# Chunked scan: head states packed into 112 rows by 96 channels, with the states' outputs computed by two row tiles

## The chip, the cores and the metric

The kernel runs on one core of a Trainium2 chip. A core has five engines that work side by side and wait for each other through semaphores: TensorE (PE, matmuls from SBUF into PSUM), VectorE (DVE), ScalarE (ACT), GpSimd (POOL, which in this kernel works on SBUF only) and SyncE (SP, which here issues nearly all transfers). PSUM is used in eight banks of 512 fp32 values per partition. The metric is the device time of one launch in microseconds, for a batch of eight images. The kernel before took 30100.37 us (median of 3 runs, 30061.18 to 30136.38).

## The reference, cut to what matters

Four layers work on x of shape (8, 64, 64, 96), each as `x = x + layer(group_norm(x))`. Layers 0 and 2 are selective scans, layer 3 is a spectral layer. The change concerns layer 1 alone, a chunked scan over the 4096 tokens in four directions k (rows, columns, and both reversed), with 6 heads of 32 channels (192 in all) and a state of 16 values. For one chunk of tokens t, s and one head h:

```python
cum  = cumsum(dt * A)                              # per head, within the chunk
Wt   = (C[t] . B[s]) * tril(exp(cum[t]-cum[s])) * dt[s]
y_intra = einsum('bctsh,bcshd->bcthd', Wt, xr)
S_loc   = einsum('bcsh,bcshn,bcshd->bchdn', decay_end * dt, Brh, xr)
state   = exp(cum[last]) * state + S_loc           # from chunk to chunk
y_inter = einsum('bcth,bcthn,bchdn->bcthd', exp(cum), Crh, prev_states)
y = y_intra + y_inter + xr * Dp
```

So a state belongs to one head: 16 state values by that head's 32 channels. The products of one head's state values with another head's channels are never used.

## The kernel before, in words

The batch is worked image by image, and an image layer by layer. `chunked_scan` (L711) does layer 1: the convolution, then two orders (`chunked_order`, L744), o = 0 for row order and o = 1 for column order, each with its forward and its reversed direction (i = 0 and 1). So the code below runs 16 times in a launch. Chunks have Q = 128 tokens, so an order has 32 chunks per direction.

The first half of an order ("turn") projects B, C and dt, transposes x into `xt` (tokens on partitions) and so on. The second half (from L843) is the chunk loop. Its order of work is written out by hand (`tc.manual_schedule()`): what a step emits is what each engine executes, in that order. Step n works on two items at once, the forward chunk n and the reversed chunk 31 - n, and each stage runs ahead of the next (L1075 to L1085):

- `decays(n+1)`, ACT: for each item, absolute value and exponential of `sg` in PSUM (L952, L953), which gives `wt` in SBUF, 128 x 768; POOL makes `xdt` (L957).
- `outputs(n)`, PE: for each item and each half of the channels (hf), three matmuls `wt`, `xdt` into 32-row column groups of `py` (L1022), and then one matmul of the state with `ce` that is added to the same 96 rows (L1030). `py` is one bank.
- `shares(n+1)`, PE: for each item one matmul, `bw` (6 heads x 16 state values, 96 columns) by all 192 channels of `xt` (L972) into `st`, 96 x 192. This computes every head against every channel.
- `sums(n+2)`, PE: four matmuls into `sg` (L936), by row tiles of 32 rows, one of each item side by side; POOL makes `bw` (L924). `sg` has two buffers of two banks, one for each item, so that these matmuls need the exponentials of `decays(n+1)` done.
- parts of two "quads". A quad prepares what four chunks need, in four parts that are run in four successive steps: `pl` (PE, L872); then its copy `lr` (ACT, L881), `rr` (POOL, L883) and `cb` (PE, L892); then `cbm` (DVE, L895) and `pd` (PE, L899); then `ec` (ACT, L904) and `ce` (POOL, L906). `pl`, `cb` and `pd` take turns in a pool of two banks (L847). In the steady part of the loop a step with `pd` and `pl` alternates with a step with `cb`. The last four steps of an order have no quad part that uses PE.
- `weights(n+1)`, DVE: `wt` times `cbm` for each item (L984).
- `add_y(n)`, DVE: adds `py` into y (L1046 in the first half of order 0, else L1060).
- `advance(n+1)`, DVE: for each item `own` = `st` times a mask that keeps each head's own channels (L1001), and the new state = old state times the chunk's decay plus `own` (L1003), both 96 x 192. The state that `outputs` uses is that of the `advance` of the step before.

The state's rows are (head, state value) and its columns all 192 channels, with zeros where the head of the row isn't that of the channel, so that one matmul of all 96 rows gives the sum over heads.

`py`, `st` and `xdt`: `py` and `st` have a single buffer, so `outputs(n+1)` waits for `add_y(n)`, and `shares` for the `own` of the step before. The eight banks are: quad pool two, `sg` four, `py` one, `st` one.

Of the kernel before, what the change touches and what calls it, by code (L numbers as in the profile page):

```python
# [9 lines left out]
F32 = mybir.dt.float32  # L10
# [7 lines left out]
DM = 96  # L18
NST = 16
# [8 lines left out]
Q = 128  # L28
NQ = L // Q
HID = 384  # L30


C_IN = 0
# [21 lines left out]
K_LW = K_UB + 128  # L55
K_DIA = K_LW + 2 * LWC
K_S6 = K_DIA + 6
K_BLK = K_S6 + 4 * 96
K_UP = K_BLK + 192
K_DN = K_UP + 128  # L60
K_ALL = K_DN + 64

# [2 lines left out]
def tile_vision_stack(  # L65
# [645 lines left out]
    def chunked_scan(w, d, u, y):  # L711

        xproj = w[:, C_XP : C_XP + K * 2 * XR].rearrange("p (k j r) -> p k j r", k=K, j=2)
        yr = y.rearrange("p j (h w) -> p j w h", w=64)
        with tc.tile_pool(name="both", bufs=1) as bo, tc.tile_pool(name="bcd", bufs=1, space=DRAM) as bdp:
            cc = bo.tile([128, K_UP - K_TF], F32, name="cc")
            nc.sync.dma_start(cc, consts[:, K_TF:K_UP])
            lw_fixed = cc[:, K_LW - K_TF : K_DIA - K_TF].rearrange("p (i r) -> p i r", i=2)
            lw = bo.tile([128, 2, NQ, LWC], F32, name="lw")  # L730
            for i in range(2):
                (nc.gpsimd.tensor_copy if i else nc.vector.tensor_copy)(
                    lw[:, i, :, :], lw_fixed[:, i : i + 1, :].to_broadcast([128, NQ, LWC])
                )

            bts = [bo.tile([DM, 4 * Q], F32, name=f"bt{n}") for n in range(2)]
            for bt in bts:
                nc.gpsimd.memset(bt, 0.0)
            bcds = [bdp.tile([32, L], F32, name=f"bcd{k}") for k in range(K)]
            for o in range(2):  # L740
                with tc.tile_pool(name="order", bufs=1) as op:
                    chunked_order(o, w, d, xproj, u, y, yr, cc, lw, bts, bcds, op)

    def chunked_order(o, w, d, xproj, u, y, yr, cc, lw, bts, bcds, op):  # L744
        def part(at, n):
            return cc[:, at - K_TF : at - K_TF + n]

        tris = (part(K_TF, 128), part(K_TB, 128))
        past = (part(K_UF, 128), part(K_UB, 128))
        heads = part(K_DIA, RK)  # L750
        sel6 = part(K_S6, 4 * 96).rearrange("p (j m) -> p j m", j=4)
        same = part(K_BLK, 192)[:DM]
        xt = op.tile([128, NQ, 192], F32, name="xt")
        xd = op.tile([128, NQ, 2, RK + NST], F32, name="xd")
        dt = op.tile([128, NQ, 2, RK], F32, name="dt")
# [87 lines left out]
        with (  # L843
            tc.tile_pool(name="quad", bufs=3) as qp,
            tc.tile_pool(name="chunk1", bufs=4) as cp,
            tc.tile_pool(name="state1", bufs=3) as stp,
            tc.tile_pool(name="p_quad", bufs=2, space=PSUM) as pqp,  # L847
            tc.tile_pool(name="p_seg", bufs=2, space=PSUM) as psg,
            tc.tile_pool(name="p_y", bufs=1, space=PSUM) as pyp,
            tc.tile_pool(name="p_st", bufs=1, space=PSUM) as pst,  # L850
# [2 lines left out]
            quads = {}  # L853
            count = [0]

            def quad(i, base):

                m = quads[i, base] = {}
                here = slice(base * Q, (base + 4) * Q)
                src = bcds[o + 2 * i]  # L860
                bt = bts[count[0] % 2]
                count[0] += 1
                nc.sync.dma_start(bt[:NST], src[:NST, here])

                cr = qp.tile([DM, 4 * Q], F32, name="cr", bufs=2)
                for h in range(RK):
                    nc.sync.dma_start(cr[NST * h : NST * h + NST], src[NST:, here])

                pl = pqp.tile([128, 2, 256], F32, name="pl", tag="quad")
                for part, at in ((0, RK), (1, 0)):  # L870
                    for j in range(4):
                        nc.tensor.matmul(  # L872
                            pl[32 * j : 32 * j + 32, part, :Q],
                            lw[:, i, base + j, at : at + 32],
                            tris[i],
                            start=True,
                            stop=True,
                        )
                yield
                m["lr"] = lr = qp.tile([128, 2, Q], F32, name="lr", bufs=4)  # L880
                nc.scalar.copy(lr, pl[:, :, :Q])  # L881
                m["rr"] = rr = qp.tile([128, RK, Q], F32, name="rr")
                nc.gpsimd.tensor_mul(  # L883
                    rr,
                    lr[:, 1:2, :].to_broadcast([128, RK, Q]),
                    heads.unsqueeze(2).to_broadcast([128, RK, Q]),
                )

                cb = pqp.tile([128, 4, Q], F32, name="cb", tag="quad")
                for j in range(4):  # L890
                    at = slice(j * Q, j * Q + Q)
                    nc.tensor.matmul(cb[:, j, :], bt[:, at], cr[:, at], start=True, stop=True)  # L892
                yield
                m["cbm"] = cbm = qp.tile([128, 4, Q], F32, name="cbm", bufs=4)
                nc.vector.tensor_mul(cbm, cb, tris[i].unsqueeze(1).to_broadcast([128, 4, Q]))  # L895

                pd = pqp.tile([128, 4, Q], F32, name="pd", tag="quad")
                for j in range(4):
                    nc.tensor.matmul(  # L899
                        pd[:DM, j, :], sel6[:, j, :], lr[:, 0, :], start=True, stop=True  # L900
                    )
                yield
                m["ec"] = ec = qp.tile([DM, 4, Q], F32, name="ec")
                nc.scalar.activation(ec, pd[:DM], AF.Exp)  # L904
                m["ce"] = ce = qp.tile([DM, 4, Q], F32, name="ce", bufs=4)
                nc.gpsimd.tensor_mul(ce, ec, cr.rearrange("p (j t) -> p j t", j=4))  # L906

            items = []
# [54 lines left out]
            def shares(n):  # L963

                if "bw" not in live[n]:
                    return
                st = pst.tile([DM, 2, 192], F32, name="st")
                for e in (n, n + 1):
                    i, c = items[e]
                    it = live[e]  # L970
                    it["st"] = st[:, i, :]
                    nc.tensor.matmul(  # L972
                        st[:, i, :],
                        it["bw"].rearrange("p h n -> p (h n)"),
                        xt[:, c, :],
                        start=True,
                        stop=True,
                    )

            def weights(n):  # L980
                for e in (n, n + 1):
# [8 lines left out]
            def advance(n):  # L990
                for e in (n, n + 1):
# [1 line left out]
                    m, j, it = quads[i, c - c % 4], c % 4, live[e]  # L993
                    it["before"] = states[i]
                    if "st" in it:
                        new = stp.tile([DM, 192], F32, name=f"state{i}")
                        if states[i] is None:
                            nc.vector.tensor_mul(new, it["st"], same)
                        else:
                            own = stp.tile([DM, 192], F32, name="own", bufs=1)  # L1000
                            nc.vector.tensor_mul(own, it["st"], same)  # L1001
                            last = Q - 1 if i == 0 else 0
                            nc.vector.scalar_tensor_tensor(  # L1003
                                new,
                                states[i],
                                m["ec"][:, j, last : last + 1],
                                own,
                                ALU.mult,
                                ALU.add,
                            )  # L1010
                        states[i] = new

            def outputs(n):
                py = pyp.tile([DM, 2, 2, Q], F32, name="py")
                for e in (n, n + 1):
                    i, c = items[e]
                    m, j, it = quads[i, c - c % 4], c % 4, live[e]
                    it["py"] = py[:, i, :, :]
                    for hf in range(2):
                        for q in range(3):  # L1020
                            h = 3 * hf + q
                            nc.tensor.matmul(  # L1022
                                py[32 * q : 32 * q + 32, i, hf, :],
                                it["xdt"][:, h, :],
                                it["wt"][:, h, :],
                                start=True,
                                stop=it["before"] is None,
                            )
                        if it["before"] is not None:
                            nc.tensor.matmul(  # L1030
                                py[:, i, hf, :],
                                it["before"][:, 96 * hf : 96 * hf + 96],
                                m["ce"][:, j, :],
                                start=False,
                                stop=True,
                            )
# [202 lines left out]
def _constants():  # L1239
# [15 lines left out]
        c[edge, K_LW + i * LWC + 2 * RK : K_LW + i * LWC + 3 * RK] = 1  # L1255
    h = np.arange(RK)
    c[:, K_DIA : K_DIA + RK] = (m[:, None] % 32 < 2 * RK) & (m[:, None] % 32 % RK == h)
    for j in range(4):
        c[:, K_S6 + 96 * j : K_S6 + 96 * j + 96] = r == 32 * j + s[:, :96] // NST
    c[:DM, K_BLK : K_BLK + 192] = r[:DM] // NST == np.arange(192)[None, :] // 32  # L1260
    c[:DM, K_GRP : K_GRP + 96] = (r[:DM] // 3 == s[:, :DM] // 3) / 3.0

    f = np.minimum(m, 128 - m)
# [120 lines left out]
```

## Time and profile before

| | us |
|---|---|
| median of 3 runs | 30100.37 (30061.18 to 30136.38) |
| the profiled execution | 30160.23 |
| its span, first to last instruction | 30158.4 |
| busy over the span: PE, DVE, POOL, ACT | 23685.8, 24821.0, 21704.5, 16367.5 |
| mean granted TensorE clock | 0.754 |
| L1022 on PE, `wt` and `xdt`, x12288 | 854.5 busy |
| L1030 on PE, state and `ce`, x3968 | 920.2 busy |
| L972 on PE, `bw` and `xt`, x1984 | 410.3 busy |
| L1003 on DVE, new state, x960 | 575.7 busy |
| L1001 on DVE, own share, x960 | 335.8 busy |

A group of the profile is named by line, engine and operation, then output and inputs; "busy" is the time in which at least one of its instructions ran. An fp32 matmul of the code stands as two instructions in the trace (the 3968 rows of L1030 are 1984 calls). Ends of matmuls are modelled and overlap, so what a matmul takes of PE is read from one start to the next. A "window" is a stretch of the span in us. The chunk loops of the first image lie at about 1531 to 1736 us and 1797 to 2004 us; the other seven images repeat them.

### The profile page before, as it was taken

What the parts mean: (1) busy time and instruction counts of PE and PEld (TensorE: products, weight loads), DVE (VectorE), ACT (ScalarE), POOL (GpSimd) and SP (SyncE); (2) the same over time, 40 slices, a digit from 0 to 9 for tenths busy, and PEclk for the clock granted to TensorE, in tenths of its full rate; (3) what the DMA queues carried; (4) which work ended last, traced back from release to release, by engine and by line L of the source; (5) the groups of instructions that cost most, each with busy time, mean ns of one, the idle gap of its engine ahead of it and who ended that gap; (6) DMA issues with size and microseconds to landing.
All of it is one profiled execution on the core that took longest, in us unless ns stands there. A gap on an engine that the chain in (4) does not pass through costs nothing. (4 is left out here: it accounts for less than half of the span.)

```text
span 30158.4 us, 279416 instructions
## 1 busy us (share of the span) xinstructions
PE 23685.8 (79%) x90246; PEld 8903.9 (30%) x90246; DVE 24821.0 (82%) x17921; ACT 16367.5 (54%) x28493; POOL 21704.5 (72%) x8844
## 2 busy tenths in 40 slices
PE   7797877978779787797877978779787797877978
PEld 1141412414124141241412414124141241412414
DVE  9879698796987969879698796987969879698796
ACT  5546465464654646546465464654646546465464
POOL 8749487594875948759497594975949759487594
PEclk7687777867768777787777877768777687776877
DMA  5415253152541525415253152531525315253152
GB/s 124 96 35 132 61 124 92 38 131 59 123 94 37 132 58 123 95 37 132 61 123 92 40 132 57 124 92 40 132 58 124 92 39 131 58 124 93 38 132 60
DMA packets 1503971, 2689.40 MB, mean 89 GB/s; under 512 B 305624, under 2 KB 313144, under 8 KB 1502512
## 3 DMA queue, kind: packets, MB, share of 16 engines
q1 hardware_dynamic: 1485872, 2665.23, 37.6%
q8 instruction: 723, 11.85, 0.2%
q10 hardware_dynamic: 16640, 6.29, 0.1%
q14 instruction: 736, 6.03, 0.1%
HBM read 2287.51 MB, written 383.06 MB: 89 GB/s over the span
## 5 line engine op out<-in xcount | busy, mean ns | idle before, releaser
L569 DVE TENSOR_TENSOR_SCAN h<-da,db 128x1026 f32<-128x1026 f32 x6144 | 13729.5, 2281 | 504.0 <-PE py L607 163.8
L590 POOL TENSOR_TENSOR h<-h,c 128x2048 f32<-128x2048 f32 x3072 | 12746.6, 4175 | 146.6 <-ACT state L585 142.4
L533 PE MATMUL pu<-du,cst 32*128 32x512 f32 x4096 | 3240.4, 881 | 3524.5 <-DVE db L539 3499.4
L554 ACT ACTIVATE da<-dx,a0s 128x512 f32<-128x512 f32 x6144 | 4243.4, 691 | 2592.1 <-DVE h L569 2431.3
L554 ACT ACTIVATE da<-dx,a2s 128x512 f32<-128x512 f32 x6144 | 4243.5, 691 | 2589.6 <-DVE h L569 2433.0
L607 PE MATMUL py<-h,cst 128*32 128x512 f32 x24576 | 5415.8, 811 | 68.0 <-POOL h L590 68.0
L539 POOL TENSOR_TENSOR db<-du,b 128x2048 f32<-128x2048 f32 x1024 | 4650.6, 4542 | 580.1 <-ACT db L525 580.1
L539 DVE TENSOR_TENSOR db<-pu,b 128x2048 f32<-128x2048 f32 x2048 | 4642.2, 2267 | 6.3 <-issue 6.3
L607 PEld LDWEIGHTS py<-h,cst 128*32 128x32 f32 x24576 | 1180.7, 145 | 4967.1 <-issue 4529.5
L229 POOL TENSOR_SCALAR xn<-xs,sb 96x512 f32<-96x512 f32 x192 | 203.1, 1062 | 3191.2 <-DVE sb L209 3050.5
L533 PEld LDWEIGHTS pu<-du,cst 32*128 32x128 f32 x4096 | 802.0, 243 | 5542.9 <-DVE db L539 3999.3
L455 PE MATMUL pv<-u,wk 96*128 96x512 f32 x2048 | 1774.1, 1008 | 760.9 <-ACT raw L451 760.9
L446 PE MATMUL pv<-u,wk 96*96 96x512 f32 x2048 | 1480.9, 852 | 515.3 <-ACT state L585 245.0
L597 PE MATMUL py<-y,cst 96*96 96x512 f32 x1536 | 1551.1, 1108 | 403.8 <-ACT raw L460 363.6
L952 ACT ACTIVATE sg<-sg 128x768 f32<-128x768 f32 x1024 | 820.5, 801 | 1400.3 <-PE sg L936 1400.3
L498 POOL TENSOR_TENSOR du<-raw,u 96x512 f32<-96x512 f32 x1024 | 1442.2, 1430 | 0.0
L984 DVE TENSOR_TENSOR wt<-wt,cbm 128x768 f32<-128x768 f32 x1024 | 1022.9, 1004 | 492.1 <-ACT wt L953 491.8
L585 ACT COPY state<-h 128x4 f32<-128x4 f32 x3072 | 607.6, 198 | 1157.3 <-DVE h L569 1157.3
L1146 DVE SCALAR_TENSOR_TENSOR f<-p,w3bs,f 128x512 f32<-128x512 f32 x768 | 576.7, 751 | 719.6 <-ACT f L1139 693.0
L906 POOL TENSOR_TENSOR ce<-ec,cr 96x512 f32<-96x512 f32 x256 | 405.0, 1582 | 976.2 <-ACT ec L904 966.0
L455 PEld LDWEIGHTS pv<-u,wk 96*128 96x128 f32 x2048 | 535.8, 289 | 1921.9 <-ACT raw L451 1444.1
L883 POOL TENSOR_TENSOR rr<-lr,cc 128x768 f32<-128x768 f32 x256 | 375.7, 1468 | 1001.2 <-ACT lr L881 813.5
(210 smaller groups left out, 32525.8 us busy)
## 6 DMA issues: line engine op xcount, KB each, us to landing
dx<-dd SPq DMA_DIRECT2D x4096, 192.0 KB, 3.8
b<-bcd SPq DMA_DIRECT2D x2048, 256.0 KB, 5.2
c<-bcd SPq DMA_DIRECT2D x2048, 256.0 KB, 6.5
du<-dud SPq DMA_DIRECT2D x2048, 128.0 KB, 2.7
dd<-raw SPq DMA_DIRECT2D x1024, 192.0 KB, 5.3
dud<-du SPq DMA_DIRECT2D x512, 128.0 KB, 1.9
xd<-xs SPq DMA_DIRECT2D x256, 192.0 KB, 2.1
xs<-xd SPq DMA_DIRECT2D x128, 384.0 KB, 5.7
```

Source lines behind the costliest of these rows:

```text
L446: nc.tensor.matmul(pv[:DM], weights[k][:, hi, 128:], uv[hi], start=(hi == 0), stop=(hi == 1))
L455: nc.tensor.matmul(pv, weights[k][:, hi, :128], uv[hi], start=(hi == 0), stop=(hi == 1))
L498: nc.gpsimd.tensor_mul(cut(du[:, hf, :], wh), cut(delta[hf], wh), uv[hf])
L533: nc.tensor.matmul(pu, sel[rows, :], m["du"][rows, n // 3, :], start=True, stop=True)
L539: (nc.gpsimd if pool else nc.vector).tensor_mul(groups(m["db", n]), (m["du2"][:, n // 3, :] if pool else m["pu"]) .unsqueeze(1) .to_broadc ...
L554: nc.scalar.activation(dst[:, g, :LC], made[i]["dx"][n // 3][:, n % 3, :], AF.Exp, scale=av4[:, k, n, gs : gs + 1],)
L569: nc.vector.tensor_tensor_scan(made[i]["h", n][:, at][:, way], das[p][:, rev : 2 * SEG + rev][:, way], made[i]["db", n][:, at][:, way], 0. ...
L590: nc.gpsimd.tensor_mul(h, h, made[i]["c"])
L597: nc.tensor.matmul(py, skip[:, hf, :] if k == 0 else ident[:DM, :DM], view((u if k == 0 else y)[:, hf, :], wh, c * LC, LC), start=True, st ...
L607: nc.tensor.matmul(py[32 * q : 32 * q + 32, :], red, hs[q][:, g, :], start=False, stop=(g == NSG - 1),)
L952: nc.scalar.activation(sg, sg, AF.Abs)
L984: nc.vector.tensor_mul(it["wt"], it["wt"], m["cbm"][:, j : j + 1, :].to_broadcast([128, RK, Q]),)
```

## The change

States become 112 rows by 96 channels. Rows 0 to 47 hold heads 0 to 2 (channels 0 to 95), rows 64 to 111 hold heads 3 to 5 (channels 96 to 191), and rows 48 to 63 stay zero. With that:

- `shares` makes four matmuls in place of two: for each item and half 48 columns of `bw` by that half's 96 channels, into rows 0 to 47 and 64 to 111.
- `advance` works on 112 x 96 in place of 96 x 192.
- `outputs` makes all six `wt`/`xdt` matmuls of an item first, and then two matmuls of state and `ce`, each of 48 rows (0 to 47, and 64 to 111), into the two halves of `py`, which now lie in two different banks.
- `ec`, `ce`, `pd`, `cr` and `bt` get the same 112 rows (`cr` becomes a pair of fixed buffers, cleared once per image, as `bt` was), by constants that are laid out anew.
- The banks are shared out anew: `py` has two; `st` and `pl` lie in one bank together (`pst2`, cleared once per order by DVE); `cb` and `pd` have one bank between them (`bufs=1`).

The diff, cut to its core:

```diff
-            bts = [bo.tile([DM, 4 * Q], F32, name=f"bt{n}") for n in range(2)]
-            for bt in bts:
-                nc.gpsimd.memset(bt, 0.0)
+            bts = [bo.tile([HR, 4 * Q], F32, name=f"bt{n}") for n in range(2)]
+            crs = [bo.tile([HR, 4 * Q], F32, name=f"cr{n}") for n in range(2)]
+            for t in bts + crs:
+                nc.gpsimd.memset(t, 0.0)
...
-            tc.tile_pool(name="p_quad", bufs=2, space=PSUM) as pqp,
+            tc.tile_pool(name="p_quad", bufs=1, space=PSUM) as pqp,
...
+            pst2 = pst.tile([128, 512], F32, name="pst2")
+            nc.vector.memset(pst2, 0.0)
+            sts = pst2[:HR, :192].rearrange("p (i c) -> p i c", i=2)
+            pl = pst2[:, 256:].rearrange("p (a t) -> p a t", a=2)
...
-                pl = pqp.tile([128, 2, 256], F32, name="pl", tag="quad")
...
-                        pd[:DM, j, :], sel6[:, j, :], lr[:, 0, :], start=True, stop=True
+                        pd[:HR, j, :], sel6[:, j, :], lr[:, 0, :], start=True, stop=True
...
-                    it["st"] = st[:, i, :]
-                    nc.tensor.matmul(
-                        st[:, i, :],
-                        it["bw"].rearrange("p h n -> p (h n)"),
-                        xt[:, c, :],
-                        start=True,
-                        stop=True,
-                    )
+                    it["st"] = sts[:, i, :]
+                    for hf in range(2):
+                        nc.tensor.matmul(
+                            sts[64 * hf : 64 * hf + 48, i, :],
+                            it["bw"].rearrange("p h n -> p (h n)")[:, 48 * hf : 48 * hf + 48],
+                            xt[:, c, 96 * hf : 96 * hf + 96],
+                            start=True,
+                            stop=True,
+                        )
...
-                            own = stp.tile([DM, 192], F32, name="own", bufs=1)
+                            own = stp.tile([HR, 96], F32, name="own", bufs=1)
...
-                py = pyp.tile([DM, 2, 2, Q], F32, name="py")
+                py = pyp.tile([DM, 2, 4 * Q], F32, name="py")
+                py = py.rearrange("p j (i t) -> p j i t", i=4)
...
+                    for hf in range(2):
                         if it["before"] is not None:
+                            rows = slice(64 * hf, 64 * hf + 48)
                             nc.tensor.matmul(
-                                py[:, i, hf, :],
-                                it["before"][:, 96 * hf : 96 * hf + 96],
-                                m["ce"][:, j, :],
+                                py[:, hf, i, :],
+                                it["before"][rows, :],
+                                m["ce"][rows, j, :],
                                 start=False,
                                 stop=True,
                             )
```

## The prediction

> **What bounds the kernel now.** I first asked where the code of the change runs and which engine is never idle there. The windows view of two stretches inside the chunk loops of one image, one of each order (columns: us, then busy time and instructions of PE, PE's weight loads, DVE, ACT, POOL, then granted clock, DMA share, GB/s):
>
> ```profile
> 1604.00:1655.00 51.00, 51.00 (x481) 31.66 (x480) 40.83 (x82) 27.91 (x41) 30.47 (x41) 1.00 0.09 20
> 1844.00:1895.00 51.00, 51.00 (x481) 31.63 (x481) 42.98 (x69) 27.91 (x41) 30.32 (x41) 1.00 0.08 20
> ```
>
> The page's whole-span averages (DVE 82%, PE 79%) hide this: here PE is busy 51.00 of 51.00 us at full clock, DVE 80 to 84%, ACT 55%, POOL 60%. A busy PE can be one that crawls, so next I read PE's timeline over one pair of steps (start us, us to the modelled end of the last, what; no line carries a bracket with idle time):
>
> ```profile
> 1603.29 0.42 PE L1022 MATMUL py<-wt,xdt 128*32 128x128 f32 x6
> 1603.64 0.46 PE L1030 MATMUL py<-ce,state 96*96 96x128 f32 x2
> 1604.03 0.42 PE L1022 MATMUL py<-wt,xdt 128*32 128x128 f32 x6
> ...
> 1606.15 0.82 PE L972 MATMUL st<-xt,bw 128*96 128x192 f32 x4
> 1606.89 1.56 PE L936 MATMUL sg<-rr,lr 32*128 32x384 f32 x8
> 1608.38 1.11 PE L899 MATMUL pd<-lr,cc 128*96 128x128 f32 x8
> 1609.43 0.64 PE L872 MATMUL pl<-cc,lw 128*32 128x128 f32 x16
> 1609.89 0.40 PE L1022 MATMUL py<-wt,xdt 128*32 128x128 f32 x6
> ...
> 1614.96 1.16 PE L892 MATMUL cb<-cr,bt 96*128 96x128 f32 x8
> 1616.05 0.31 PE L1022 MATMUL py<-wt,xdt 128*32 128x128 f32 x3
> ```
>
> From start to start: the step with `pd` and `pl` takes 6.60 us, the one with `cb` 6.16, the pair 12.76. Single starts repeat to 0.01 us from group to group, which waiting on another engine would not do. So each us taken off PE here is gained, until the next ring of waits binds. The last four steps of an order, without quads, take 5.10 us each. An order has 13 pairs, one short first step and those four; there are 16 orders.
>
> The next limit is seen on the other two engines in the same pair, ACT and DVE (in brackets the idle time before, and what ended it):
>
> ```profile
> 1608.48 0.80 ACT L952 ACTIVATE sg<-sg 128x768 f32<-128x768 f32 x1 [3.00 <-PE sg L936]
> ...
> 1610.86 0.81 ACT L953 ACTIVATE wt<-sg 128x768 f32<-128x768 f32 x1
> ...
> 1610.16 0.96 DVE L984 TENSOR_TENSOR wt<-wt,cbm 128x768 f32<-128x768 f32 x1 [0.83 <-ACT wt L953]
> 1611.70 0.96 DVE L984 TENSOR_TENSOR wt<-wt,cbm 128x768 f32<-128x768 f32 x1 [0.59 <-ACT wt L953]
> 1612.93 1.12 DVE L1046 SCALAR_TENSOR_TENSOR y<-u,d,py 96x128 f32<-96x128 f32 x4 [0.27 <-PE py L1030]
> 1613.97 0.35 DVE L1001 TENSOR_TENSOR own<-st,cc 96x192 f32<-96x192 f32 x1
> 1614.42 1.02 DVE L1003 SCALAR_TENSOR_TENSOR state<-state,ec,own 96x192 f32<-96x192 f32 x1
> ```
>
> ACT waits 3.00 us for PE's sums. ACT's ring is: sums' start to first absolute value 1.59 us (1606.89 to 1608.48), four activations 3.19 (to 1611.67), about 0.07 hand-over to the next sums: 4.85 us per step.
>
> **What the Trainium skill says.** TensorEngine Tiling, Key Properties: changing the tiling mode drains the array. The trace agrees: the last L1022 start to the first L1030 start is 0.202 us, where a 128-column pass without a mode change takes 0.109. TensorE: Matmul & The Clock Gate, LDWEIGHTS: a load costs its columns over 1.2 GHz, so 80 ns for 96; in the trace the second pass after a mode change comes at 0.187, that is 0.109 + 0.078. The same page, The mechanism: tiles on different rows run side by side. L936 does it here with 32-row tiles: two 384-column passes start 7 ns apart and the next two 0.322 later, the time of one. No row shows 64-row tiles. SBUF — State Buffer, section "SBUF: two separate sides": DVE and POOL share a port pair as an exclusive lock; L1003 fits it, with 0.415 us median, 0.600 mean and 1.672 at most.
>
> **The change part by part.**
>
> Outputs. Now an item costs 2 x (0.35 + 0.39) = 1.48 us: four mode changes. After: six L1022 matmuls are four bursts of three passes, which by the bursts of `pl` start at 0, 0.134, 0.243, 0.352, the last pass at 0.366; mode change 0.202; two passes of both row tiles side by side, 0.187 + 0.007; mode change 0.202. Sum 0.964 per item, 1.93 per step.
>
> Shares. Four 192-column passes now take 0.162 each; with the mode change before the sums, 0.74 from 1606.15. After: 96-column passes, by the slope between 128 (0.109) and 192 columns (0.162), 0.082. Two column tiles side by side make four pairs: 0.122 with the first load of 48 columns, 0.082, 0.082, 0.007, then 0.175 to the sums: 0.47.
>
> Outputs and shares together: 3.60 now (1603.29 to 1606.89), 2.40 after: 1.20 to 1.21 us per step. `pd` with 112 weight columns and `cb` with 112 rows keep their passes.
>
> The pair on PE alone: 12.76 - 2.42 = 10.34. Against ACT's 2 x 4.85 = 9.70 PE still binds. In the four steps without quads PE would need 3.89, so ACT binds: 4.85, a gain of 0.25 each.
>
> DVE. `own` and the new state lose 96 elements per row. The slope from `own` (192 elements, 0.35) to L984 (768, 0.96) is 1.07 ns per element, so 0.10 us each, 0.40 per step. Alone this is off the path.
>
> New waits. In the built program dependences in `pst2` are held for the bank, not the columns. So in the step with `pl`, DVE's first `own` waits for `pl`, the last work of PE's step; behind it on DVE stand the other three of `advance`, then the next step's L984 twice and L1060, and for that `outputs` waits (`py` has one buffer). That closes a ring, per pair: from the end of `pl`, `advance` 1.23 (1.63 now from 1607.70 to 1609.33 on DVE, less 0.40), two L984 2.0, add 1.1 to 1.2, hand-overs 0.15; then PE's outputs 1.93, shares 0.47, sums 1.49, `pd` 1.04, `pl` 0.36 to its last start and 0.28 to its end. Sum 10.1 to 10.2, just under PE's 10.34, with nothing for the port lock. With the mean of L1003, 0.2 to 0.4 more: 10.3 to 10.6. I take 10.55 for the pair.
>
> The single quad bank: `pd` waits for `cbm`, `cb` for `ec`. In the steady loop `cbm` ends at 1604.7 and `pd` starts at 1608.38, so 3.7 us cover it; `cb` waits for `ec` already with two banks, since three tiles rotate. Before the loop `pd` starts at 1525.92 and `cbm` ends at 1526.86: about 1.0 us later, once per order, on the path. ACT's `lr` and the `own` of the other step wait for each other's reads with over a us to spare. `rr` and `ce` follow `ec` and `lr` at 1.5 us each on POOL and are needed 1.6 us or more later. Two more 0.52 us clears on POOL lie before 96.69 us of its idling; that of `pst2` is on DVE while it waits for PE.
>
> Sum per order: 13 x (12.76 - 10.55) = 28.7; four steps 1.0; first step 0.3; start -1.0: 29.0 us. Times 16: 464 us. The profiled execution (30160) becomes 29696; the median of the runs lies 60 below it, so 29636, say 29640.
>
> What no row prices: which bank the next order's first matmuls wait for (`py`'s second bank is freed last), -2 to +2 us per order, so up to 32 us each way; I take 0.
>
> **The rivals.**
>
> *The row tiles don't overlap.* Then the state matmuls cost 2 x 0.109 more per item, 0.44 per step; the gain per step falls to 0.77. For it: no 64-row tile in the trace. Against it: L936. 26 x 0.77 + 1.3 - 1.0 = 20.3 per order: 29775.
>
> *DVE becomes the bound* by the ring above. If one state update in each `advance` is stretched (2.52 us from 1613.97 to 1616.49 now, 2.1 after) and L984 pairs take 2.2 (2.12 at 1604.62), add 1.3: 5.6 + 5.57 + 0.15 = 11.3 per pair, 1.46 gained: 19.3 per order, 29790. For it: POOL's work falls on a shorter step. Against it: the stretch hits some steps only.
>
> *Slower.* The 64-row tiles are run one after the other with repeated passes and loads. The change loses once the two tiles of an item take over 0.605 us more than the 0.39 I give them, about 1.0 (now two separate matmuls take 0.78). At 1.2 a step is 0.41 longer: 26 x 0.41 x 16 = 170, 30270. Against it: L936 costs no extra.
>
> *No effect*, since PE isn't the bound: the windows exclude it.
>
> **How the numbers follow.** Likeliest 0.66 (29540 to 29720, from a pair of 10.34 with the unpriced end of the order in its favour and 40 us of run spread, to one of 10.8), no overlap 0.12, DVE 0.15, slower 0.04, no effect 0.03. The range takes in both faster rivals: 29540 to 29840. About 0.3% (90 us) is what a measurement of this kernel can tell from no change; all three faster cases are beyond it: faster 0.93, within 0.03, slower 0.04.
>
> **What would show it.** PE's timeline: an outputs item of about 0.96 us with one pair of state passes 7 ns apart, shares of 0.47, steps of 5.2 to 5.4 and 5.0 to 5.2. In a run with serial tiles the passes start 0.109 apart. On DVE `own` waits for `pl` every second step; if L1022 is then seen waiting for DVE's add, the ring binds. ACT's wait for sums falls from 3.0 to about 1.7 us or less. Wrong would be an unchanged start distance of 0.39 behind L1030, or PE idle in the windows.

## The result, and the profile after

The changed kernel takes 29754.24 us (median of 4 runs, 29741.47 to 29794.88) against 30086.37 us for the kernel before on the same chip (4 runs, 30061.18 to 30136.38). The ratio is 0.989, with a 95% interval of 0.9873 to 0.9907. The forecast was 29640 with a range of 29540 to 29840, faster: direction and range held, and the time is 114 us above the number. By the medians of this chip the gain is 332 us, where the forecast had 460 from its own median. The profiled execution took 29741.47 us, with a span of 29739.6. From profiled execution to profiled execution (30160.23 to 29741.47) the gain is 419 us, where the working of the forecast has 464: 45 of the 114 us are missing in the traces. The other 69 or so are the step from a profiled execution to a median: the forecast took 60 us off, as before's own runs stood to its profile, and the profiled execution of the changed kernel happens to lie 13 us below its median.

The windows view of the two stretches inside the chunk loops that the prediction read (columns: window, us, then busy time and instructions of PE, PE's weight loads, DVE, ACT, POOL, then granted clock, DMA share, GB/s), for the kernel after:

```profile
1604.00:1655.00 51.00, 49.43 (x619) 32.22 (x620) 48.06 (x94) 34.36 (x49) 36.59 (x47) 1.00 0.10 23
1844.00:1895.00 51.00, 50.85 (x622) 32.83 (x613) 48.83 (x84) 34.15 (x50) 40.20 (x47) 1.00 0.10 24
```

In the same 51 us PE now runs 619 and 622 matmuls where it ran 481 (a pair of steps now has 128 of them, where it had 120), and it is no longer busy for the whole of the time. DVE has gone from 40.83 and 42.98 us busy to 48.06 and 48.83: it is nearly full, though it was given less to do in each step.

PE's timeline over one undisturbed step and the next one (start in us, us to the modelled end of the last, what; a bracket is idle time before it and what ended it):

```profile
1592.18 0.64 PE L1030 MATMUL py<-wt,xdt 128*32 128x128 f32 x12
1592.74 0.46 PE L1040 MATMUL py<-ce,state 48*96 48x128 f32 x4
1593.14 0.64 PE L1030 MATMUL py<-wt,xdt 128*32 128x128 f32 x12
...
1594.10 0.54 PE L978 MATMUL pst<-xt,bw 128*48 128x96 f32 x8
1594.57 1.56 PE L942 MATMUL sg<-rr,lr 32*128 32x384 f32 x8
...
1597.14 0.64 PE L1030 MATMUL py<-wt,xdt 128*32 128x128 f32 x12
...
1600.97 0.54 PE L978 MATMUL pst<-xt,bw 128*48 128x96 f32 x8 [1.84 <-DVE own L1007]
```

From one L1030 start to the next an outputs item takes 0.96 us (1592.18 to 1593.14) where it took 1.48; from L978 to L942 the shares take 0.47 where they took 0.74; the step takes 4.96 us. PE's own work came out as forecast. The last line is what did not: PE waits 1.84 us for `own`, on which the same matmuls (L972) never waited in the kernel before. In all that is 38.9 us (next view, L978).

The groups that carry the change, in the groups view of the kernel after (busy us, mean ns of one, then idle time before and what ended it):

```profile
L958 ACT ACTIVATE sg<-sg 128x768 f32<-128x768 f32 x1024 | 819.2, 800 | 845.9 <-PE sg L942 845.9
...
L1009 DVE SCALAR_TENSOR_TENSOR state<-state,ec,own 112x96 f32<-112x96 f32 x960 | 687.5, 716 | 35.7 <-DVE own L1007 0.5
L1030 PE MATMUL py<-wt,xdt 128*32 128x128 f32 x12288 | 679.9, 288 | 71.8 <-DVE y L1070 56.0 <-DVE y L1056 11.6
...
L978 PE MATMUL pst<-xt,bw 128*48 128x96 f32 x3968 | 271.6, 258 | 38.9 <-DVE own L1007 38.9
...
L1007 DVE TENSOR_TENSOR own<-pst,cc 112x96 f32<-112x96 f32 x960 | 243.6, 254 | 104.6 <-PE pst L878 82.5
```

ACT's wait for the sums has fallen from 1400.3 us to 845.9. PE's `outputs` (L1030) wait 67.6 us for DVE's add into y, where L1022 waited 4.3: that is the sign which the prediction had named for a ring that binds. `own` is shorter, 254 ns where it was 350. The state update, which got half the elements per row, takes more time than before: 687.5 us in all against 575.7, a mean of 716 ns against 600. That is the odd number of this result. The updates of both kernels, counted by their durations:

| 960 state updates | up to 0.6 us | 0.6 to 1 us | 1 to 2 us | 2 to 3 us | over 3 us | shortest, longest |
|---|---|---|---|---|---|---|
| before (L1003) | 665 | 160 | 135 | 0 | 0 | about 0.41, 1.672 |
| after (L1009) | 559 | 164 | 191 | 30 | 16 | about 0.32, 4.293 |

Where the time of a long update goes is seen by setting three engines beside each other, at one of the sixteen. DVE:

```profile
1570.81 3.92 DVE L1009 SCALAR_TENSOR_TENSOR state<-state,ec,own 112x96 f32<-112x96 f32 x1
1574.77 0.26 DVE L1007 TENSOR_TENSOR own<-pst,cc 112x96 f32<-112x96 f32 x1
```

POOL in the same stretch:

```profile
1570.67 1.46 POOL L889 TENSOR_TENSOR rr<-lr,cc 128x768 f32<-128x768 f32 x1
1572.10 0.97 POOL L963 TENSOR_TENSOR xdt<-xt,dt 128x192 f32<-128x192 f32 x2
1573.03 0.65 POOL L930 TENSOR_TENSOR bw<-xd,d_end 128x96 f32<-128x96 f32 x2
1573.64 0.97 POOL L963 TENSOR_TENSOR xdt<-xt,dt 128x192 f32<-128x192 f32 x2
1575.69 1.37 POOL L930 TENSOR_TENSOR bw<-xd,d_end 128x96 f32<-128x96 f32 x2 [1.07 <-PE pst L978]
```

And PE:

```profile
1575.17 0.54 PE L978 MATMUL pst<-xt,bw 128*48 128x96 f32 x8 [1.83 <-DVE own L1007]
1575.64 2.39 PE L942 MATMUL sg<-rr,lr 32*128 32x384 f32 x8
```

The update starts at 1570.81, while POOL is in `rr`. Six more POOL instructions follow without a gap, the last ends at about 1574.61, and the update ends at 1574.73. Then the second `own` can run, and PE's `shares`, which need its bank read, come 1.83 us late. When PE resumes, L942 takes 2.39 us where it takes 1.56: in the 7 us from 1575 the granted clock is 0.59. This step takes 9.44 us where its neighbours of the same kind take 5.40. The next long update, which ends at 1600.53, costs PE the same 1.84 us and is followed by full clock, and that step takes 7.71. The windows view of the stretches after the two waits (the clock is the third number from the right):

```profile
1575.00:1582.00 7.00, 6.83 (x54) 4.51 (x56) 4.70 (x12) 3.31 (x5) 1.37 (x2) 0.59 0.02 4
1601.00:1605.00 4.00, 3.78 (x45) 2.47 (x48) 3.96 (x10) 1.94 (x3) 1.37 (x2) 1.00 0.00 0
```

The slow clock is not a single case. In the trace's record of the granted clock it falls to 0.50 at thirteen places in the middle steps of o = 0 (steps 2 to 27 of an order), for 3.4 or 6.8 us in nearly all of them. Together that takes 37 us of full-clock time. It never falls in the middle steps of o = 1, nor in those of any other run of this document.

To place the gain, I took the chunk loops apart by the starts of `outputs` in each trace: per order the 26 middle steps (13 pairs), then the last four. Means over the eight images, in us:

| | o = 0, 26 steps | o = 1, 26 steps | last four, o = 0 / 1 | mean pair |
|---|---|---|---|---|
| before | 165.4 | 165.4 | 20.4 / 23.7 | 12.72 |
| after | 147.1 (144.2 to 152.3) | 137.8 (136.3 to 138.6) | 18.8 / 22.1 | 10.96 |

Summed over the 16 orders the middle steps give 367 us and the last four 25. From the last outputs of o = 0 to the first of o = 1 the path got 2.4 us longer, 20 us in all eight images. So the chunk loops give about 374 us. The other 44 of the 419 lie on the way from one image's chunk loops to the next one's, nearly all of it in layers that the change doesn't touch, and are luck of the two executions: that way varies from 3292 to 3319 us in both kernels alike, so totals of equal kernels differ by tens of us, and the loop's own steps are the finer measure below. In the middle steps of the changed kernel PE waits 60 us in o = 0 and 18 us in o = 1, where it waited 1 us in all in the kernel before.

### The profile page after: what moved, and what is told of

Its sections match the earlier page's. It is cut to its first block, busy times and chain, and to the rows that moved or that the text cites. A ratio compares the mean times of both kernels' runs of the same rounds, so it can differ in the third digit from the quotient of the medians.

```text
span 29739.6 us, 283816 instructions
## 1 busy us (share of the span) xinstructions
PE 23171.7 (78%) x92230; PEld 8658.8 (29%) x92230; DVE 24783.7 (83%) x17937; ACT 16367.9 (55%) x28493; POOL 21831.6 (73%) x8860
## 5 line engine op out<-in xcount | busy, mean ns | idle before, releaser
L230 POOL TENSOR_SCALAR xn<-xs,sb 96x512 f32<-96x512 f32 x192 | 204.6, 1070 | 3154.4 <-DVE sb L210 3015.9
L958 ACT ACTIVATE sg<-sg 128x768 f32<-128x768 f32 x1024 | 819.2, 800 | 845.9 <-PE sg L942 845.9
L296 POOL TENSOR_SCALAR xn<-xs,sb 96x512 f32<-96x512 f32 x192 | 151.6, 791 | 1242.1 <-issue 893.3
L1149 ACT ACTIVATE f<-p,lin,w3bs 128x512 f32<-128x512 f32 x768 | 597.0, 777 | 830.5 <-PE p L1146 810.5
```

What stands on the lines that cost most here:

```text
L958: nc.scalar.activation(sg, sg, AF.Abs)
```

## The experiments

The theory was **A**: what is missing is time that DVE's state update stands still while POOL works, because two of its operands are in SBUF, and a step in which it stands long makes PE wait. The rivals were **B**, the ring that the prediction had priced (`own` waits for `pl`, since both lie in one bank), and **C**, that the change did less on PE than it seems, so that the gain comes from shorter DVE work or from the banks rather than from the row tiles.

### The own share stays in PSUM

```diff
-                            own = stp.tile([HR, 96], F32, name="own", bufs=1)
-                            nc.vector.tensor_mul(own, it["st"], same)
+                            own = it["st"]
+                            nc.vector.tensor_mul(own, own, same)
```

The masked product is written back over `st`, so the update has one tensor in SBUF and one in PSUM. One thing comes with it: PE's next `shares` now wait until the update has read the bank, where they waited for `own` alone.

> The changed kernel, but the masked share is written back into its own PSUM bank instead of an SBUF tile, so that the state update reads one operand from SBUF and one from PSUM, not two from SBUF. Theory A (the shortfall is the state update locked out while GpSimd works without a gap): the state update's longest case falls from 4.3 us to under 1, no shares wait for VectorE for 1.8 us any more, the 26 middle steps of an order of the first kind fall from 147 to 138-139 us, total 29660 to 29700. Theory B (the shortfall is the wait of the own share for pl in the shared bank): nothing changes, 29740 to 29770.

Measured: 29635.69 us (29598.55 to 29684.13), ratio to the kernel before 0.9841, interval 0.9826 to 0.9855. This interval lies wholly below that of the changed kernel (0.9873 to 0.9907), so this version beats both kernels. The middle steps take 134.6 us (o = 0) and 136.75 (o = 1), a mean pair of 10.44, and every image has the same to 0.1 us. That is better than expected: 24 us below the range in time, and 134.6 in o = 0 where 138 to 139 was expected. The groups view of this kernel:

```profile
L1009 DVE SCALAR_TENSOR_TENSOR state<-state,ec,pst 112x96 f32<-112x96 f32 x960 | 302.1, 315 | 34.9
...
L1007 DVE TENSOR_TENSOR pst<-pst,cc 112x96 f32<-112x96 f32 x960 | 252.5, 263 | 168.9 <-PE pst L878 152.0
```

Not one of the 960 updates is stretched (longest 317 ns, where it was 4293), while POOL's work is the same. `own` now waits longer for `pl`, 152.0 us against 82.5, since DVE is done earlier. In o = 0 that costs nothing, PE is full again; in o = 1 it is not quite:

```profile
1604.00:1655.00 51.00, 50.99 (x633) 33.52 (x626) 44.21 (x93) 34.59 (x50) 39.22 (x50) 1.00 0.10 23
1844.00:1895.00 51.00, 50.40 (x616) 32.76 (x616) 46.83 (x84) 33.74 (x48) 38.77 (x47) 1.00 0.10 24
```

So the stretched update is the cause of the missing part of the loop. The 109 us between the middle steps' sums (476 saved against 367) is the price of it: 100 in o = 0 and 9 in o = 1. Of the 100, PE's waits are 60 and the slow clock that follows some of them is 37.

### `pl` ahead of `pd`

```diff
-                for _, key in sorted(parts.get(n, ()), key=lambda x: x[0]):
+                for _, key in sorted(parts.get(n, ()), key=lambda x: x[0] in (-2, -1)):
```

PE makes `pl` before `pd` in the steps that have both, so `own` can start 1.06 us earlier; `cb` and `ec` keep their order. This takes rival B's wait away and leaves the update's operands in SBUF.

> The changed kernel with one swap: in the steps that have both, pl is emitted before pd, so that the own share is released about 1 us earlier. Theory A: the long stalls stay, the steps with pl fall from 5.65 to 5.40 us in the second order of each image; total 29710 to 29740. Theory B: the middle steps of both orders come near 13 x 10.35 = 135 us, total about 29640.

Measured: 29685.03 us (29640.50 to 29715.89), ratio 0.9855, interval 0.984 to 0.987; middle steps 136.4 and 139.0 us. The groups view:

```profile
L1009 DVE SCALAR_TENSOR_TENSOR state<-state,ec,own 112x96 f32<-112x96 f32 x960 | 617.2, 643 | 35.6 <-DVE own L1007 0.5
...
L1007 DVE TENSOR_TENSOR own<-pst,cc 112x96 f32<-112x96 f32 x960 | 242.3, 252 | 31.2 <-PE pst L878 11.7
```

Both theories missed here. The wait for `pl` is nearly gone, as B says, yet o = 1 did not gain (139.0 against 137.8): PE still waits 22.5 us for DVE's add in its middle steps, so that wait alone is not what bounds that order. And o = 0 gained 10.7 us although the update's operands are where they were, which A as I had put it excludes. The trace shows what changed there. The longest update is now 2284 ns: one that starts a microsecond earlier meets other POOL instructions, and none stands for 3 or 4 us. But 104 updates of o = 0 still take over 1 us (128 in the changed kernel), while PE's waits in its middle steps fall from 60 us to 5 and the clock stays at 1.00. So there are two readings: the edit moved the two engines' phases, or the microsecond of slack covers the stretches that are left. This run doesn't separate them. Either way, an edit that does nothing about the operands can take most of the stretch's cost away.

### Both edits

The two edits above together.

> The share in PSUM and pl before pd together. Theory A with the ring as second limit: every pair of steps near 10.35 to 10.4 us, 26 steps 135 to 136 us in both orders, total 29620 to 29660, faster than both kernels. Theory B: as pl before pd alone.

Measured: middle steps 135.6 us in both orders, mean pair 10.43; 29677.94 us (29612.26 to 29687.89), ratio 0.9848, interval 0.9832 to 0.9865. The mean pair is that of the first edit alone (10.44), but two effects cancel in it. With `pl` ahead of `pd` the step that has both takes PE 5.51 us where it took 5.40, without any wait, and o = 0, which had no wait left, gets 1.0 us longer. In o = 1 PE's waits for DVE's add, 13.3 us in the middle steps of the eight images with the first edit alone, are nearly gone (1.2 for all waits), and this order gets 1.15 us shorter. PE is now full there:

```profile
1844.00:1895.00 51.00, 51.00 (x625) 32.96 (x626) 47.60 (x85) 34.48 (x49) 37.28 (x50) 1.00 0.11 24
```

So with the update unstretched, rival B's wait still costs o = 1 about 0.12 us per pair, and the swap costs PE about as much. The median is 18 us above the range that was expected, and 42 above that of the first edit alone, with overlapping intervals. The loops don't explain this: 75 of the 76 us between the two profiled executions lie on the ways from image to image.

### The kernel before with its own share in PSUM

```diff
-                            own = stp.tile([DM, 192], F32, name="own", bufs=1)
-                            nc.vector.tensor_mul(own, it["st"], same)
+                            own = it["st"]
+                            nc.vector.tensor_mul(own, own, same)
```

> The kernel before with only the masked share written back into PSUM. Theory A: the lock-outs were there before but TensorE, the bound, didn't feel them; the state update's mean falls from 0.60 to about 0.42 us and the time stays within 0.3% of the kernel before. If lock-outs cost time before too, it falls by 50 us or more.

Measured: 30136.78 us against 30122.26, ratio 1.0001 (0.9993 to 1.001). The groups view:

```profile
L1003 DVE SCALAR_TENSOR_TENSOR state<-state,ec,st 96x192 f32<-96x192 f32 x960 | 393.3, 410 | 42.2 <-DVE st L1001 0.5
```

The update is flat here too, 410 ns and at most 413, 182 us of DVE's time less than before's 575.7. None of it reaches the end: the middle steps take 165.4 us as they did, as expected. The stretch was in the kernel before, under the cover of a PE that never waits. The change took the cover away.

### The state's matmul right after each half

```diff
-                    for hf in range(2):
```

(the second of the two loops over the halves in `outputs`, so that each half's state matmul follows its own three `wt`/`xdt` matmuls, as in the kernel before; shares, states and banks stay as changed).

> The changed kernel with the old order in the outputs: three matmuls of one half, its state matmul, then the other half, so the two 48-row tiles never stand next to each other and the tiling mode changes four times per item. By the prediction's working an item goes back from 0.96 to 1.48 us, a step up by 1.03, a pair to 12.4 us: 26 steps 161 us, total 30040 to 30090, nearly the whole gain gone. If the gain came from the shares, the smaller updates or the banks, it stays under 29850.

Measured: 30103.35 us (30059.62 to 30157.76) against 30107.6, ratio 0.9998 (0.9989 to 1.0006). PE's timeline of one such item:

```profile
1605.36 0.42 PE L1030 MATMUL py<-wt,xdt 128*32 128x128 f32 x6
1605.71 0.46 PE L1039 MATMUL py<-ce,state 48*96 48x128 f32 x2
1606.10 0.42 PE L1030 MATMUL py<-wt,xdt 128*32 128x128 f32 x6
...
```

A half takes 0.35 + 0.39 us as in the kernel before: 48 rows are no cheaper than 96 when the tile runs alone. Middle steps take 160.4 us in both orders, a pair 12.34. So what is left of the change (smaller shares and states, the banks, 112 rows) is worth 0.38 us per pair, 80 us in all, of which the way between the two orders takes 32 back (77.8 us in place of 73.8, in eight images); the total shows no difference (48 us would lie outside its interval, so some of it is lost outside the middle steps in a way that isn't shown). Together with the run before this one, in which DVE was relieved without any effect, that is the end of rival C: the gain of the change hangs on the order of PE's eight matmuls. Whether that order would do as much without the rest of the change was not tested.

### All 112 rows in each state matmul

```diff
-                            rows = slice(64 * hf, 64 * hf + 48)
+                            rows = slice(0, HR)
```

A test of time alone: each half's state matmul takes all 112 rows, so it also adds the other half's states. The order of the matmuls is that of the changed kernel, and the two no longer run side by side (their passes start 0.109 us apart in the trace).

> The changed kernel with the new order, but each of the two state matmuls takes all 112 rows (each half then adds the other half's states too, so this is a test of time alone): they need the whole array and can't run side by side. By the prediction's working an item costs two passes of 0.109 us more, 1.18 us, a step 0.42 more, a pair 11.2: 26 steps 146 to 149 us, total 29820 to 29880. If the grouping alone gives the gain and the tiles don't overlap, nothing changes: 29740 to 29770.

Measured: 29807.26 us (29782.43 to 29874.15) against 30107.6, ratio 0.9905 (0.9887 to 0.9924), middle steps 145.6 and 147.5, a pair of 11.27. PE's timeline:

```profile
1603.17 0.61 PE L1030 MATMUL py<-wt,xdt 128*32 128x128 f32 x12
1603.71 0.68 PE L1040 MATMUL py<-ce,state 112*96 112x128 f32 x4
1604.32 0.64 PE L1030 MATMUL py<-wt,xdt 128*32 128x128 f32 x12
...
```

From the start of L1040 to the next L1030 it is 0.61 us, against 0.40 when the two tiles run side by side. So the overlap is worth 0.21 per item, 0.84 per pair, as 11.27 - 10.44 = 0.83 says against the kernel with `own` in PSUM (0.85 in o = 0, where PE waits in neither). The time is 13 us below the range that was expected. The rest of the gain on outputs, from 1.48 us to 1.15 or 1.18 per item, comes of putting the matmuls of a kind together, which leaves two of four mode changes. In total this kernel loses little against the changed one (0.9905 against 0.989, with overlapping intervals): at its slower step the updates are stretched less, 577.4 us in all against 687.5, about as in the kernel before.

### POOL's `bw` computed twice

To see whether a fuller POOL makes the stretches longer, I had POOL compute `bw` twice into the same tile (the changed kernel, then the one with `own` in PSUM). The letters B and C in these two expectations name other rivals than above: B that only the update's place among the steps matters, C that POOL's products come late.

```diff
-                        nc.gpsimd.tensor_mul(
+                        for _ in range(2):
+                            nc.gpsimd.tensor_mul(
```

> The changed kernel with POOL's bw computed twice (the same values into the same tile): 0.65 to 0.94 us more per step on POOL, whose busy share of a steady stretch goes from 0.67 to about 0.80; everything else is as in the changed kernel. Theory A (the long state updates are DVE shut out by POOL's instructions that follow each other without a gap): with fewer gaps more updates take over 2 us (46 of 960 now, expected 80 or more) and their sum rises above 687 us to 800 or more; the 26 middle steps rise from 147/138 us to 150 to 165 in both orders; time 29800 to 30000. Theory B (it is the place of the update among the steps that matters, not how full POOL is): no change, 147/138 us, 29750. In both, a long update ends within about 0.13 us after the end of a POOL instruction.

> The same doubling of bw on the kernel that keeps own in PSUM, so that the state update has one operand in PSUM. Theory A: the update stays at 312 to 318 ns, POOL's fuller schedule costs the path nothing or little, 26 middle steps 135 to 139 us, time 29630 to 29700. Rival C (POOL's products themselves come late for PE and ACT when POOL has more to do): it loses as much as the changed kernel does by the same doubling, and PE or ACT is seen waiting for bw, xdt, rr or ce.

Measured for the changed kernel with `bw` twice: 29734.9 us (29705.52 to 29763.90), ratio 0.9865 (0.985 to 0.988), middle steps 140.3 and 140.0. Its windows and groups views (L1010 is the update here):

```profile
1604.00:1655.00 51.00, 49.61 (x590) 32.12 (x586) 48.71 (x91) 32.70 (x46) 45.74 (x65) 1.00 0.10 25
```

```profile
L1010 DVE SCALAR_TENSOR_TENSOR state<-state,ec,own 112x96 f32<-112x96 f32 x960 | 681.8, 710 | 35.6 <-DVE own L1008 0.5
```

My expectation failed. POOL's busy time in the window went from 36.59 to 45.74 us of 51, and the updates' sum stayed (681.8 against 687.5). Sixty-seven take over 2 us in place of 46, but only one takes over 3. Order 0 is 7 us faster than with less work on POOL, order 1 two slower. So the length of a stretch does not go with how full POOL is. "No change" is as wrong: the added instructions moved the phases, of the sixteen updates over 3 us one is left, and with them went the slow clock: it is 1.00 in all middle steps, where it had cost o = 0 37 us.

With `own` in PSUM, `bw` twice gave 29710.11 us (29688.56 to 29753.24), ratio 0.9858 (0.9841 to 0.9874), 10 us above the range that was expected. The middle steps hold at 135.8 and 136.2 us, and the update at 315 ns, even with POOL busy for 49.51 of 51 us. What was lost came elsewhere: the last four steps went from 18.9 and 22.2 us to 23.4 and 25.2, where steps are shortest; in this kernel PE's state matmul is seen waiting 28.6 us for `ce` of POOL, for which it had not waited in the changed kernel. That is the sign of this expectation's rival C.

One more reading bears on what ends a stretch. Of the 237 updates over 1 us in the changed kernel, nineteen in twenty end between 0.11 and 0.14 us after the end of a POOL instruction, and in none of the sixty longest is it more than 0.2. The sixteen longest end where POOL then stands still for a microsecond or more. Nearly all the other long ones end between two POOL instructions that follow each other directly, and there the second takes some 18 ns longer than usual (523 ns against 505 for `xdt`). In the kernel before, every update over 0.6 us got in at the first such boundary after it had waited 0.4 us; in the changed kernel up to seven boundaries passed. What decides whether DVE gets in at a boundary wasn't settled by these runs. That POOL is the other side rests on these ends and on the page named below: no run took POOL's work away.

## Why the prediction was right, and where its sum was off

**The time.** 29754 lies in the range, but above the band that was called likeliest (29540 to 29720), and it is nearer to the numbers of two rivals (29775 without overlap, 29790 with DVE as the bound) than to 29640. The time alone could not have told the three apart; the traces and the runs do. The 44 us that came from other layers helped it by luck.

**What bounds the kernel.** Right. With DVE's update unstretched, 2.28 of the 2.42 us taken off PE per pair are gained (12.72 to 10.44), and PE is full again in o = 0 (50.99 of 51.00). One argument for it does not hold: that single starts repeat to 0.01 us doesn't exclude waits. In o = 1 of the kernel with `own` in PSUM every image's middle steps agree to 0.1 us, though PE waits for DVE there.

**Outputs and shares.** Right to 0.01 us: 0.96 for an item (0.964 forecast), 0.47 for the shares (0.47). The PE-only pair of 10.34 stands in the trace wherever nothing disturbs it: 5.40 + 4.94 us. The overlap of two 64-row tiles, for which no row of the trace of before spoke, is real, and so the rival without it and the one that is slower fell. The run with all rows gave it as 0.21 us per item, the 2 x 0.109 that the rival would have lost.

**The ring through `own` and `pl`.** The wait is there as described, 82.5 us in 126 instances, and so is the sign that the ring binds (L1030 waiting for DVE's add). What it costs differs by order. With the update stretched, taking the wait away gave order 0 10.7 us and order 1 nothing; with the update unstretched, it costs order 0 nothing and order 1 about 0.12 per pair. The price of 10.1 to 10.2 without the lock, under PE's 10.34, is borne out in order 0 (134.6 / 13 = 10.35) and a little low for order 1 (10.52).

**The port lock: the step that failed.** The prediction added "0.2 to 0.4" per pair for it, from the mean of L1003, and took 10.55. Order 1 comes near that number (137.8 / 13 = 10.60), in part by luck: with the update unstretched it still takes 10.52, because of the ring. Order 0 doesn't: 147.1 / 13 = 11.32, which is the DVE rival's 11.3, though by another course than that rival's (one update in each `advance` stretched a little, in every step). What happens is that most steps are as short as forecast and a few very long: in the first image's order 0 four steps take 6.6 to 9.4 us, in the fourth image's seven take 6.1 to 9.4. Per pair this is 0.77 more in order 0 than forecast, 13 x 0.77 x 8 = 80 us. A mean of 600 ns and a longest of 1672 described the phases of the old schedule. Its successor's are others, with up to 4293, and a ring with 0.2 us of slack has little to set against such a wait. For the slow clock after a wait of PE the prediction had no term at all: that is 37 us, nearly half of what order 0 fell short by. The Trainium skill, SBUF — State Buffer, section "SBUF: two separate sides", says that when a VectorE instruction has two inputs in SBUF and GpSimd reads SBUF too, the one that starts first holds the shared ports for its whole instruction, and the other is blocked. In the trace of before a stretched update waited for the end of one POOL instruction, which agrees. In the changed kernel the block lasted through up to eight instructions on end, so that the measured 3.92 and 4.29 us go beyond what that page and the old trace gave reason to price.

**Smaller terms.** The pair of 12.76 is right for twelve pairs of an order, the thirteenth takes 12.30: 7 us too much gain in all. The start of an order, from its first `pl`, was forecast 1.0 us later: it is 0.1 earlier in order 0 and 0.7 later in order 1. The four last steps gave 1.6 us per order where 1.0 was forecast. The unpriced way from one order to the next, taken as 0 with a range of -2 to +2, cost 1.7 us between the orders of an image; what the second bank of `py` has to do with it was not tested.

**The base.** The sum was made against an execution of 30160 and moved by 60 to the median. One execution is no base for 60 us: other layers, which both kernels share, vary by that much, and here the changed kernel's profile lay on the other side of its median.

## What to carry to other kernels

When PE stops being the bound, stalls of other engines that it covered come onto the path with their longest durations, not their means: look at the spread of every instruction on the next ring, and ask what it shares with whom. A wait of PE can also cost more than its own length, as the slow clock shows here. In this kernel the VectorE instruction with both tensors in SBUF, beside a busy GpSimd, was such a one; leaving one operand in PSUM cost 9 ns on the instruction before it and removed the spread. And put PE's matmuls of one tile shape together: here 1.90 of the 2.28 us gained per pair hang on that order (12.34 to 10.44), not on the smaller work.

## What the runs showed that was not expected

- A DVE update of 0.32 us stood for up to 4.293 us, across as many as eight POOL instructions that followed each other without a gap, and with one operand in PSUM never for more than 0.317.
- More work on POOL (36.6 to 45.7 us busy of 51) made the kernel with the stretched updates no slower (0.9865 against 0.989).
- After PE had stood for 1.83 us, its granted clock was 0.59 over the next 7 us at one place, and 1.00 after 1.84 us at another, 26 us later in the same order. All changes of the clock in this trace lie on one raster of 3.413 us, to 0.01 us. The first wait falls whole into one stretch of the raster (1572.81 to 1576.22), the second is split by a boundary at 1600.12 into 0.98 and 0.86 us. Over all middle steps of the changed kernel the clock fell after each of the twelve stretches with 1.48 us or more of idle PE and after none of the twenty with 0.86 to 1.23 us. It fell once after 0.73 us, so PE's idle time in a stretch is not the whole of it.
- A matmul of 48 rows and one of 96, each alone in its mode, take PE the same 0.39 us up to the next start; two of 48 rows in two row tiles take 0.40 together, mode change included.
